# Own taps of a row LSTM as three products, with new gate blocks and a new written order

## The chip, the cores and the metric

The kernel runs on one core of a Trainium2 chip. The core has a matrix engine (TensorE, PE in the profile, with PEld for its weight loads), a vector engine (VectorE, DVE), an activation engine (ScalarE, ACT), a general engine (GpSimd, POOL) and a queue that starts DMAs (SyncE, SP). Each engine works off its own list of instructions in the order in which they stand, and waits at its head on semaphores that the other engines raise. The metric is the device time of one execution in microseconds (us); for the kernel before it is 1970.99 us (median of 3 runs, 1969.05 to 1977.06).

## The reference

A group normalisation of the input is followed by a row LSTM: a masked convolution of each image row gives the input part of four gates, a 3-tap convolution of the previous row's hidden state gives the other part, and the result is added to the input.

```python
# x: (8, 96, 128, 128); W_is: (384, 96, 1, 3); W_ss: (384, 96, 3)
# mask: tap 2 is zero; of tap 1 the first third of the outputs sees inputs 0:32,
# the second third 0:64, the last third all 96; tap 0 is whole
its = conv(group_norm(x), W_is * mask)          # along the row, padding 1
def step((h, c), row_in):                       # one image row, h and c (8, 96, 128)
    gates = conv(h, W_ss) + row_in              # 3 taps along the row
    g5 = gates.reshape(B, 3, 4, 32, 128)        # 3 thirds of channels, 4 gates
    f, i, o = sigmoid(g5[:, :, 0]), sigmoid(g5[:, :, 1]), sigmoid(g5[:, :, 2])
    g = tanh(g5[:, :, 3])
    c = f * c + i * g
    h = o * tanh(c)
    return (h, c), h
out = x + moveaxis(scan(step, (0, 0), rows of its), 0, 2)
```

All of it is 32-bit floating point.

## The kernel before

**Two half-steps in flight.** The 8 images are two groups s = 0, 1 of 4. One half-step n is one image row of one group; there are 256, and consecutive half-steps belong to different groups, so that one can be in its products while the other is in its gates. A row of 128 pixels is held as 64 even and 64 odd pixels; 4 images by 64 pairs make the 256 columns of nearly every instruction.

**Products.** The 384 gate channels are three blocks A, B, C of 128, each in a bank of PSUM (tiles `ps0`, `ps1`, `ps2`), with the even pixels in the first half of a bank and the odd ones in the second. The three taps of the hidden state are four products per block for two pixels: `1` (moving operand `vs`, the sum of even and odd h) and `2` (`vf`, their difference), then `0` and `3` (`vd`, differences with the neighbours). The input part has three more: `P`, `Q`, `E`, from the group's 64 own input channels in `xs`; the other 32 channels lie beside h in the rows of the h products. After `1`, `2`, `P`, `Q` come for each block `cp` (ACT copies the first half of the bank with the bias to `m`, line 569), `lo` (DVE: first half = m + second, line 573) and `hi` (DVE: second half = m - second, line 577). `0` and `E` are added on top of the first half, `3` on top of the second.

**Lanes.** A matmul of 128 rows is cut into two pieces of 64 rows, and each piece into two instructions of 64 output columns, so that four 64x64 tiles of the array work at once (`n_split`, line 453, and `mm`, line 485). The two row halves are called lanes here; a bank may be written by one lane at a time, and `Lanes.wait` makes PE wait for its own earlier products when the lane changes.

**Gates.** In block A lie the 96 forget gates and a third of g, in B the input gates and a third of g, in C the output gates and the last third. `si` is a sigmoid (line 593), `ta` a tanh (line 581), `fg` the product of forget gate and cell (DVE, line 598), `gt` that of input gate and g (line 605 on POOL for even pixels, 607 on DVE for odd ones), `ce` the new cell (617), `th` its tanh (622), `ou` the new h (630), `F` and `S` the operands `vf` and `vs` (649, 645), `D` the operand `vd` (POOL, line 653), `re` the sum with the input (671).

**What sets the order.** It is written by hand. The body of the loop over half-steps 2 to 253 is the string `PERIOD` (line 781), so there are 252 bodies. In it `'` marks the previous half-step, `''` the one before that, `+` the next; `<` and `>` name a lane; each product stands twice, once for each lane; a last letter a or b means even or odd pixels. `X` and `U` normalise the shared channels of a later row block (line 320 on POOL, 318 on ACT), `W1` to `W3` widen, add and subtract the own channels (320, 337, 341 on POOL). The half-steps ahead of the loop run during the pass that loads the input for its statistics, and the last ones have a list of their own (`LAST`). Waits between engines are set from the tiles that an instruction reads and writes; a bank is one tile there.

Rows arrive through SP: `load` (line 165) brings 4 rows of a group for the residual, `load_rows` (line 157) the own channels, twice, to 64 partitions each.

## Time and profile before

| | |
|---|---|
| median of 3 runs | 1970.99 us (1969.05 to 1977.06) |
| the profiled execution's own time | 1972.7 us |
| its span, first to last instruction | 1970.9 us |
| mean granted TensorE clock | 0.999 |
| instructions | 80552 |

How to read it: busy time of an engine is the union of its instructions' times. One matmul of the program on 32-bit data is two MATMUL records, one for each pass. In a row of the timeline stand the start, the time, the engine, the line of the kernel, the operation, the tiles written and read, the shape, and in brackets how long the engine stood idle just before and what ended that; neighbouring rows of the same form are merged, with their count behind x. In a row of the groups stand count, busy time, mean ns of one, and the idle time before them.

### The profile page before, as it was taken

The numbers are of one execution on the slowest core, as the hardware profiler recorded it, in microseconds if no ns is written. First come the engines' busy times: TensorE is split into PE (matmuls) and PEld (weight loads), VectorE is DVE, ScalarE is ACT, GpSimd is POOL, SyncE is SP. The second block draws the span as 40 slices with busy tenths as digits, with TensorE's granted clock in tenths as the row PEclk, the third lists the DMA queues.
The fourth block names the chain that finished last, engine by engine and source line by source line (L and its number), as shares of the span: only waits on it lengthen the run. The fifth ranks groups of instructions, "written<-read, shape, count | busy, mean of one in ns | idle before, by whom it ended". The sixth has DMA issues, their size and how long they took to land.

```text
span 1970.9 us, 80552 instructions
## 1 busy us (share of the span) xinstructions
PE 1904.7 (97%) x34510; PEld 1686.7 (86%) x34510; DVE 1801.1 (91%) x4014; ACT 1565.9 (79%) x3501; POOL 1360.3 (69%) x1645
## 2 busy tenths in 40 slices
PE   3799999999999999999999999999999999999998
PEld 0368999999999888888888999998888888988886
DVE  5888999999999999999999999999999899999998
ACT  6688888888888888787887878887888788877786
POOL 3457777777777777777777777777777777777751
PEclk9999999999999999999999999999999999999999
DMA  9993433544444345444434444443454444344411
GB/s 402 420 306 92 111 96 85 120 112 106 99 104 109 79 112 120 98 104 98 105 84 112 117 102 98 104 106 82 114 120 98 99 104 107 85 109 118 100 35 34
DMA packets 101428, 236.83 MB, mean 120 GB/s; under 512 B 5840, under 2 KB 7376, under 8 KB 95056
## 3 DMA queue, kind: packets, MB, share of 16 engines
q1 hardware_dynamic: 101072, 231.70, 45.2%
q8 instruction: 271, 4.44, 1.0%
q14 instruction: 85, 0.70, 0.1%
HBM read 181.34 MB, written 50.33 MB: 118 GB/s over the span
## 4 chain that ended last, share of the span: by engine, by line
PE 93%; DMA 3%; ACT 2%; DVE 1%; issue 1%; POOL 0%; SPq 0%; POOLq 0%; DVEq 0%; ACTq 0%
PE ps L498 92%; DMA xs<-in_x_dram 3%; DVE bst L1119 1%; ACT xs L239 0%; ACT xs L240 0%; ACT g L581 0%; PE rows L198 0%; ACT ps L593 0%; ACT piece L239 0%; DVE hx L630 0%; PE pv L274 0%; POOL xw L320 0%; DVE c L617 0%; SPq L1106 0%; ACT xr L208 0%
## 5 line engine op out<-in xcount | busy, mean ns | idle before, releaser
L498 PE MATMUL ps<-vd,wl 64*64 64x256 f32 (+1 forms) x12096 | 1208.9, 376 | 8.0 <-issue 5.1
L498 PE MATMUL ps<-vs,wm 64*64 64x256 f32 (+1 forms) x6058 | 832.9, 376 | 3.0 <-issue 1.6
L498 PEld LDWEIGHTS ps<-vd,wl 64*64 64x64 f32 (+1 forms) x12096 | 714.2, 133 | 81.2 <-issue 11.5
L498 PE MATMUL ps<-vf,wm 64*64 64x256 f32 (+1 forms) x6058 | 777.1, 376 | 1.5 <-issue 1.2
L498 PE MATMUL ps<-xs,wx 64*64 64x256 f32 (+2 forms) x7096 | 759.0, 346 | 1.8 <-POOL xs L337 1.8
L593 ACT ACTIVATE ps<-ps 96x512 f32<-96x512 f32 (+1 forms) x768 | 388.2, 506 | 227.0 <-PE ps L498 218.6
L498 PEld LDWEIGHTS ps<-xs,wx 64*64 64x64 f32 (+1 forms) x7096 | 483.6, 133 | 17.9 <-POOL xs L337 3.3
L581 ACT ACTIVATE g<-ps 32x256 f32<-32x256 f32 (+1 forms) x1021 | 469.2, 482 | 24.3 <-PE ps L498 3.2
L498 PE MATMUL ps<-xs,wt 64*64 64x256 f32 (+1 forms) x3024 | 458.3, 376 | 0.1
L569 ACT ACTIVATE m<-ps,wl 128x256 f32<-128x256 f32 x766 | 363.0, 474 | 107.6 <-PE ps L498 81.0
L498 PEld LDWEIGHTS ps<-vs,wm 64*64 64x64 f32 (+1 forms) x6058 | 409.3, 132 | 42.0 <-POOL vs L645 2.5
L653 POOL TENSOR_TENSOR vd<-hx 128x512 f32<-128x512 f32 x257 | 287.9, 1120 | 177.2 <-DVE vs L645 168.9
L498 PEld LDWEIGHTS ps<-vf,wm 64*64 64x64 f32 (+1 forms) x6058 | 355.8, 132 | 60.9 <-DVE vf L649 1.8
L573 DVE TENSOR_TENSOR ps<-m,ps 128x256 f32<-128x256 f32 x768 | 324.2, 422 | 81.1 <-ACT m L569 74.8
L577 DVE TENSOR_TENSOR ps<-m,ps 128x256 f32<-128x256 f32 x768 | 327.1, 426 | 17.7
L671 DVE TENSOR_TENSOR x<-x,hx 96x512 f32<-96x512 f32 x253 | 341.8, 1351 | 0.0
L320 POOL TENSOR_SCALAR xw<-xr,rstd,nmr 128x512 f32<-128x512 f32 (+1 forms) x264 | 210.2, 797 | 129.1 <-DVE x L671 116.0
L320 POOL TENSOR_SCALAR hx<-x,rstd,nmr 32x512 f32<-32x512 f32 (+1 forms) x244 | 220.9, 905 | 77.6 <-POOL xs L341 52.9
L341 POOL TENSOR_TENSOR xs<-xw 128x512 f32<-128x512 f32 (+1 forms) x254 | 271.5, 1069 | 0.0
L605 POOL TENSOR_TENSOR g<-i,g 96x256 f32<-96x256 f32 x251 | 183.2, 730 | 125.6 <-ACT g L581 116.9
L498 PEld LDWEIGHTS ps<-xs,wt 64*64 64x64 f32 (+1 forms) x3024 | 210.6, 133 | 2.5 <-issue 0.9
L617 DVE TENSOR_TENSOR c<-ps,g 96x256 f32<-96x256 f32 (+1 forms) x507 | 190.9, 416 | 7.7 <-POOL g L605 0.5
(101 smaller groups left out, 1502.8 us busy)
## 6 DMA issues: line engine op xcount, KB each, us to landing
xr<-in_x_dram SPq DMA_DIRECT2D x124, 512.0 KB, 7.0
x<-in_x_dram SPq DMA_DIRECT2D x62, 768.0 KB, 7.8
out_dram<-x SPq DMA_DIRECT2D x62, 768.0 KB, 5.0
xs<-in_x_dram SPq DMA_DIRECT2D x31, 1024.0 KB, 10.9
piece<-in_x_dram SPq DMA_DIRECT2D x16, 1024.0 KB, 10.8
x<-in_x_dram SPq DMA_DIRECT2D x62, 256.0 KB, 5.4
out_dram<-x SPq DMA_DIRECT2D x2, 576.0 KB, 3.9
xs<-in_x_dram SPq DMA_DIRECT2D x2, 512.0 KB, 10.0
```

What stands on the lines that cost most here:

```text
L320: return engine.tensor_scalar(dst, src, scale, shift, ALU.mult, ALU.add)
L341: engine.tensor_sub(differences, strided(xw[:, 0, :], 0, [(W + 1, n), (J, 2), (1, J)]), strided(xw[:, 0, :], J + 1, [(W + 1, n), (0, 2), ( ...
L498: made = nc.tensor.matmul(self.ps[a][bass.ts(q, wide), bass.ts(half, HB)][:, cols], weights[rows, bass.ds(a * P + q * wide, wide)], rhs[ro ...
L569: nc.scalar.activation(self.m1[a], m1, AF.Identity, bias=column)
L573: nc.vector.tensor_add(self.ps[a][:, 0:HB], self.m1[a], self.ps[a][:, HB:])
L577: nc.vector.tensor_sub(hi, self.m1[a], hi)
L581: nc.scalar.activation(self.part(g, lo, hi, t), self.part(ps, lo, hi, t), AF.Tanh)
L593: nc.scalar.activation(to, gate, AF.Sigmoid)
L605: nc.gpsimd.tensor_mul(to, i, g)
L617: nc.vector.tensor_add(c, f, g)
L653: diff = nc.gpsimd.tensor_sub(self.operand("vd", 2)[:, :, lo:hi], strided(h, 1, [(BH * JP - 1, 2), (JP, hi - lo), (1, J)]), strided(h, 0, ...
L671: residuals.append(nc.vector.tensor_add(xo, xo, self.h))
```

## The change

The own products are laid out anew. With the even pixel e, the odd pixel o and the odd pixel of the pair to the left, the outputs are written as P (both tap weights times e, for both pixels), E (left tap times the left neighbour's difference, even pixels) and Q (centre tap times o - e, odd pixels). The centre tap is masked, so Q is made for two column halves alone: columns 64 to 127 of block A and 0 to 63 of block B, one instruction each. The rest of Q, for input channels 0 to 31, takes the 32 free rows of product `3`: `ride` (token `K`) copies those rows of Q beside the third operand. For that the gate channels are permuted (A: forget gates and a third of g; B: two thirds and a third of the input gates and a third of the output gates; C: two thirds of the output gates and of g), and the own channels become 64..95 and 0..31, the shared ones 32..63.

With it go: the gates of B are read by `iu`, `il` and `so` instead of one `si` and one `ta`; `D` becomes `Z` (128x256) and `V` (96x256); `W2` (the addition of pixels) is dropped and `W2` names the subtraction; the loads of own channels are four of 32 partitions instead of two of 64; the first rows have picking products and a bank of their own; the strings `PERIOD` and `LAST` are written anew.

```diff
+    wq = const.tile([P, 2, O4], F32, name="wq")
-    wo = [wx[:, 0, :], wx[:, 1, :], tap[3]]
...
     def load_rows(s, k, lo=0, hi=R):
-        src = rows_of(s, k, 0, C2, lo, hi)
-        for p in range(2):
-            nc.sync.dma_start(xr[s][p * C2 : (p + 1) * C2, :, lo * W : hi * W], src)
+        for p in range(4):
+            c0 = 0 if p % 2 else 64
+            nc.sync.dma_start(
+                xr[s][p * 32 : (p + 1) * 32, :, lo * W : hi * W],
+                rows_of(s, k, c0, c0 + 32, lo, hi),
+            )
...
         if i == 0:
-            first[b] = bank(f"rows{b}")
+            first[b], own_first[b] = bank(f"rows{b}"), bank(f"own{b}")
...
-    def add_pixels(xw, n, total, engine=nc.gpsimd):
-
-        engine.tensor_add(total, xw[:, 0:n, 0:J], xw[:, 0:n, J + 1 :])
...
         "1": (0, 1, ("vs", 0)),
         "2": (1, 2, ("vf", 0)),
-        "0": (0, 0, ("vd", 1)),
-        "3": (1, 3, ("vd", 0)),
+        "0": (0, 0, ("vz", 0)),
+        "3": (1, 3, ("vr", 0)),
...
+            if lane is not None:
+                lane ^= self.n % 2
+            if kind == "Q":
+                rows = lanes.take(lane=lane)
+                for a, q in ((0, 1), (1, 0)):
+                    self.images[a] = (0, BH)
+                    self.mm(a, 1, wo[kind], self.at_rows(kind), rows, (q,))
+                return True
...
-            if t == 0 and NH < self.n < last:
-                self.even_input = self.tile("i", (C, HB))
...
+        def output_gate(self, lo=0, hi=BH, t=None):
+            gate, to = self.ps[1][32:C2], self.ps[2][C2:C]
...
+        def input_upper(self, lo=0, hi=BH, t=None):
+            nc.scalar.activation(
+                self.part(self.i[0:C2], lo, hi, t), self.part(self.ps[1][C2:P], lo, hi, t), AF.Sigmoid
+            )
+
+        def input_lower(self, lo=0, hi=BH, t=None):
+            nc.scalar.activation(
+                self.part(self.i[C2:C], lo, hi, t), self.part(self.ps[1][0:32], lo, hi, t), AF.Sigmoid
+            )
...
+        def ride(self, lo=0, hi=BH):
+            nc.gpsimd.tensor_copy(
+                self.operand("vr")[C:P, 0, lo:hi], self.at_rows("Q")[C:P, lo:hi]
+            )
...
     PERIOD = (
-        "1B> 3C'< D'' 2A> 0C'< 1A> siBa' 2B< 3C'> 1B< EC'> 2C< taA' 0C'> re'' 1C< fg' taB' PB+> "
-        "PC+< cpA W1 loA cpB 1C> hiA loB hiB siBb' QCl+< taCa' taCb' EA< 2C> gtb' W2 3A< siC' "
-        "0B> gta' 0A< cpC 3B> QA+< W3 cea' tha' EB> PA+< ceb' loC 0A> 0B< oua' thb' oub' X F' "
-        "3A< 3B> QB*> S' 2A+< 2B+> 1A+< U QCh+> siA hiC"
+        "1B< U F 2A> X W1' 2B< siA' ilb' Z re'' fg' taCb' V 1C> 0C'> taA' 1B> 1A< iub' gtb' "
+        "cpB cpA 2B> 1C< 0C'< 2A< loB PC+< loA 2C< cpC hiB PB+< 0B< K+ hiA ceb' taCa' 2C> "
+        "gta' loC 0A< 3B> EA< so' siC' 0B> 3A< thb' EB> PA+> cea' hiC oub' QA> tha' EC< oua' "
+        "0A> 3C< S+ 3A> 3B< 3C> iua 1A+> ila W2'"
     )
...
     perm = np.concatenate(
-        [np.concatenate([idx[:, a].reshape(-1), idx[a, 3]]) for a in range(3)]
+        [
+            idx[k, gate]
+            for k, gate in (
+                (0, 0), (1, 0), (2, 0), (2, 3),
+                (2, 1), (2, 2), (0, 1), (1, 1),
+                (0, 2), (1, 2), (0, 3), (1, 3),
+            )
+        ]
     )
```

Two places show how the instructions stand. The names are tiles: `ps0`, `ps1`, `ps2` are the banks of blocks A, B, C, followed by group, row and a number; `wl_64`, `wm_66`, `wx_67`, `wt2_65` are weights; `x2` is the pair of column halves; in brackets is the engine whose semaphore the instruction waits for. `Lanes` is behind a wait of PE on PE.

PE before, at the end of the products `1` and `2` of half-step (row 42, group 0) with pieces of `0`, `3` and `E` of the half-step ahead of it between them:

```order
L498 MATMUL ps1_0_42_10410<-vf_0_42_10528,wm_66 64x256 [waits PE_49]
L498 MATMUL ps1_0_42_10410<-vf_0_42_10528,wm_66 64x256
L498 MATMUL ps2_1_40_10343<-vd_1_40_10430,wl_64 64x256 [waits PE_49]
L498 MATMUL ps2_1_40_10343<-vd_1_40_10430,wl_64 64x256
L498 MATMUL ps1_0_42_10410<-vs_0_42_10537,wm_66 64x256 x2
L498 MATMUL ps2_1_40_10343<-xs10_76,wt2_65 64x256 x2
L498 MATMUL ps2_0_42_10468<-vf_0_42_10528,wm_66 64x256 x2
L498 MATMUL ps2_1_40_10343<-vd_1_40_10430,wl_64 64x256 x2
L498 MATMUL ps2_0_42_10468<-vs_0_42_10537,wm_66 64x256 x2
```

Here PE waits for itself alone. PE in the changed kernel, from the last piece of `3B` of half-step (row 41, group 0) over the products `1` and `2` of (row 40, group 1) to the second pieces of `2B` and `2A`:

```order
L495 MATMUL ps1_0_41_10332<-vr_0_41_10337,wl_64 64x256
L495 MATMUL ps2_0_41_10323<-vr_0_41_10337,wl_64 64x256 [waits PE_49]
...
L495 MATMUL ps2_1_40_10444<-vs_1_40_10502,wm_66 64x256 x2
L495 MATMUL ps2_0_41_10323<-vz_0_41_10409,wl_64 64x256 [waits Activation_49]
...
L495 MATMUL ps1_1_40_10453<-vs_1_40_10502,wm_66 64x256
L495 MATMUL ps0_1_40_10485<-vs_1_40_10502,wm_66 64x256 x2
L495 MATMUL ps1_1_40_10453<-vf_1_40_10520,wm_66 64x256 [waits Activation_49]
...
L495 MATMUL ps2_0_41_10323<-vz_0_41_10409,wl_64 64x256 [waits PE_49]
L495 MATMUL ps2_0_41_10323<-vz_0_41_10409,wl_64 64x256
L495 MATMUL ps0_1_40_10485<-vf_1_40_10520,wm_66 64x256 [waits Activation_49]
```

The second pieces of `2B` and `2A` now stand behind a copy of the same bank by ACT, and the first piece of `0C` behind a tanh of bank C.

ACT before, from the copy of block C over a body's gates to the copies of A and B:

```order
L569 ACTIVATE m2_0_59_14761<-ps2_0_59_14604,wl_64 128x256 [waits PE_49]
L622 ACTIVATE th_1_57_14770<-c1_83 96x256 [waits DVE_49] x2
L593 ACTIVATE ps0_0_59_14642<-ps0_0_59_14642 96x512 [waits PE_49]
L593 ACTIVATE i_0_59_14822<-ps1_0_59_14550 96x256 [waits PE_49,Pool_49]
L581 ACTIVATE g_0_59_14836<-ps0_0_59_14642 32x512 [waits Activation_49]
L581 ACTIVATE g_0_59_14836<-ps1_0_59_14550 32x512
L569 ACTIVATE m0_1_58_14850<-ps0_1_58_14765,wl_64 128x256 [waits PE_49]
L569 ACTIVATE m1_1_58_14854<-ps1_1_58_14673,wl_64 128x256 [waits PE_49]
```

ACT in the changed kernel, from the first input gate (`iua`) to the copies of B and A; `X` is the row with L332:

```order
L622 ACTIVATE i_0_62_15646<-ps1_0_62_15467 64x256 [waits PE_49,Pool_49]
L627 ACTIVATE i_0_62_15646<-ps1_0_62_15467 32x256
L332 ACTIVATE hx10_73<-x1_16_15424,nmr1_105,rstd1_103 32x2x64 [waits DMAHW6_49,Pool_49]
L607 ACTIVATE ps0_0_62_15499<-ps0_0_62_15499 96x512
L627 ACTIVATE i_0_62_15646<-ps1_0_62_15467 32x256
L601 ACTIVATE g_0_62_15669<-ps2_0_62_15458 64x256 [waits DVE_49,PE_49]
L601 ACTIVATE g_0_62_15669<-ps0_0_62_15499 32x512 [waits DVE_49]
L622 ACTIVATE i_0_62_15646<-ps1_0_62_15467 64x256
L588 ACTIVATE m1_1_61_15684<-ps1_1_61_15587,wl_64 128x256 [waits PE_49]
L588 ACTIVATE m0_1_61_15686<-ps0_1_61_15619,wl_64 128x256 [waits PE_49]
```

The sigmoid of block A stood first of a body's gates and now stands behind two input gates of block B; seven gate instructions stand ahead of the copies, where there were four.

## The prediction

> **What bounds the kernel now.** I read the page first: the busy times, and the chain that ended last.

> ```profile
> PE 1904.7 (97%) x34510; PEld 1686.7 (86%) x34510; DVE 1801.1 (91%) x4014; ACT 1565.9 (79%) x3501; POOL 1360.3 (69%) x1645
> ...
> PE ps L498 92%; DMA xs<-in_x_dram 3%; DVE bst L1119 1%; ACT xs L239 0%; ACT xs L240 0%; ACT g L581 0%; PE rows L198 0%; ACT ps L593 0%; ACT piece L239 0%; DVE hx L630 0%; PE pv L274 0%; POOL xw L320 0%; DVE c L617 0%; SPq L1106 0%; ACT xr L208 0%
> ...
> L593 ACT ACTIVATE ps<-ps 96x512 f32<-96x512 f32 (+1 forms) x768 | 388.2, 506 | 227.0 <-PE ps L498 218.6
> ```

> 92% of the chain is products into the banks, and ACT waits 218.6 us for them before its sigmoids. Whether busy PE is full PE shows in the timeline of one body.

> ```profile
> 1003.14 0.38 PE L498 MATMUL ps<-vd,wl 64*64 64x256 f32 x2
> 1003.21 0.38 PE L498 MATMUL ps<-vf,wm 64*64 64x256 f32 x2
> 1003.36 0.38 PE L498 MATMUL ps<-vd,wl 64*64 64x256 f32 x2
> 1003.43 0.38 PE L498 MATMUL ps<-vs,wm 64*64 64x256 f32 x2
> 1003.57 0.38 PE L498 MATMUL ps<-vf,wm 64*64 64x256 f32 x2
> ...
> 1001.63 0.42 DVE L645 TENSOR_TENSOR vs<-hx 128x256 f32<-128x256 f32 x1
> 1001.97 0.42 DVE L577 TENSOR_TENSOR ps<-m,ps 128x256 f32<-128x256 f32 x1
> 1002.30 1.53 DVE L671 TENSOR_TENSOR x<-x,hx 96x512 f32<-96x512 f32 x1
> 1009.42 1.52 DVE L671 TENSOR_TENSOR x<-x,hx 96x512 f32<-96x512 f32 x1
> ```

> A lane starts a pair of records every 0.215 us (1003.14, 1003.36, 1003.57), the other lane in between; a piece of two passes holds its lane for 0.43 us and ends 0.215 + 0.38 = 0.59 us after its start. A body has 66 instructions of 64 columns, 33 to a lane pair and pass: 33 x 0.215 = 7.10 us, and the residual of one body follows that of the last after 7.12. PE never stands still, and the period is its work. The busy times of a stretch of the loop, times 7.12/400, give those of a body: DVE 6.65, ACT 5.75, POOL 5.24.

> ```profile
> 400.00:800.00 400.00, 400.00 (x7632) 365.13 (x7626) 373.50 (x843) 323.24 (x743) 294.50 (x336) 1.00 0.44 104
> ```

> **The change part by part.**

> *Products.* 66 instructions become 62 (Q two instead of six; the h products stay 48). If PE stayed full: 31 x 0.215 + 0.02 = 6.69 us, 0.43 less, over 252 bodies 108 us.

> *ACT.* These are its rows in a body, and the tail, where PE no longer covers the waits:

> ```profile
> 1001.70 0.57 ACT L593 ACTIVATE ps<-ps 96x512 f32<-96x512 f32 x1 [0.98 <-PE ps L498]
> 1002.19 0.37 ACT L593 ACTIVATE i<-ps 96x256 f32<-96x256 f32 x1
> 1002.59 1.22 ACT L581 ACTIVATE g<-ps 32x512 f32<-32x512 f32 x2
> 1004.08 1.05 ACT L569 ACTIVATE m<-ps,wl 128x256 f32<-128x256 f32 x2 [0.27 <-PE ps L498]
> 1005.02 0.37 ACT L593 ACTIVATE ps<-ps 96x256 f32<-96x256 f32 x1
> 1005.42 0.65 ACT L581 ACTIVATE g<-ps 32x256 f32<-32x256 f32 x2
> 1006.10 0.57 ACT L593 ACTIVATE ps<-ps 96x512 f32<-96x512 f32 x1
> 1006.70 0.47 ACT L569 ACTIVATE m<-ps,wl 128x256 f32<-128x256 f32 x1
> ...
> 1014.21 0.75 ACT L622 ACTIVATE th<-c 96x256 f32<-96x256 f32 x2
> 1014.99 0.50 ACT L318 ACTIVATE hx<-x,nmr,rstd 32x128 f32<-32x128 f32 x1
> ```

> ```profile
> 1958.26 0.59 PE L498 MATMUL ps<-vf,wm 128*128 128x256 f32 x2
> ...
> 1958.90 0.48 DVE L567 TENSOR_SCALAR m<-ps,wl 128x256 f32<-128x256 f32 x1 [0.62 <-PE ps L498]
> 1959.42 0.43 DVE L573 TENSOR_TENSOR ps<-m,ps 128x256 f32<-128x256 f32 x1
> 1959.88 0.43 DVE L577 TENSOR_TENSOR ps<-m,ps 128x256 f32<-128x256 f32 x1
> ...
> 1960.45 3.19 PE L498 MATMUL ps<-vd,wl 128*128 128x256 f32 x12
> ...
> 1962.28 0.57 ACT L593 ACTIVATE ps<-ps 96x512 f32<-96x512 f32 x1
> 1962.88 0.59 ACT L581 ACTIVATE g<-ps 32x512 f32<-32x512 f32 x1
> 1962.88 0.69 DVE L598 TENSOR_TENSOR ps<-ps,c 96x512 f32<-96x512 f32 x1 [0.49 <-ACT ps L593]
> ```

> An instruction of 256 columns costs 0.37 us whether it has 32 or 96 partitions, so cutting a gate by partitions adds instructions and saves nothing: per body 13 become 15, two more of 256 columns at 0.28 to 0.40 us. ACT idles 0.98 + 0.27 us in the shown body, so by load alone it would still fit 6.69. By place it does not. In the new lists there is a loop that closes once per body, and I add it up from the rows, beginning with the last piece of `3B`:

> 1. The piece ends after 0.59, and ACT starts `iua` some 0.05 later (1958.26 + 0.59 to 1958.90 is PE to DVE): 0.64.
> 2. `iua` and `ila` stand ahead of `siA` on ACT: two of 256 columns back to back, spaced 0.65 - 0.37 = 0.28: 0.56.
> 3. `siA` to `fg`: 1962.28 to 1962.88, 0.60.
> 4. `fg` 0.69 + 0.03 to `taA`, which reads the same bank: 0.72.
> 5. `taA` to `iub`: half of the 1.22 for two, 0.61.
> 6. `iub` to `cpB`: as 1002.19 to 1002.59 (a sigmoid, then another function), 0.40.
> 7. `cpB` 0.47, then the second piece of `2B` waits for it. No row shows PE released by ACT; bounds are 0.05 (PE to DVE) and 0.14 (DVE to PE, 1959.88 + 0.43 to 1960.45); I take the middle, 0.10: 0.57.
> 8. `2B` holds its lane 0.43, behind it go a piece of `0C` and that of `2A`; `2A` ends 0.59 + 0.05 later at `loA`: 1.07.
> 9. `loA` stands ahead of `hiB` on DVE and delays it by a slot, 0.34 (1001.63 to 1001.97 above, where nothing is waited for); `hiB` 0.43 + 0.10 to `0B`: 0.87.
> 10. From the first piece of `0B` to the last of `3B` its lane has seven pieces (`0A`, `E` of A, `3A`, `P` of the next half-step, `E` of C, `3C`, then `3B`): 7 x 0.43 = 3.01.

> Sum 9.05 us. `X` (0.50, one body in four, between `ila` and `siA`; next start some 0.45 later) adds 0.11: 9.16 us per body, against 6.69 of work on PE. Before, every second piece of `1` and `2` stood ahead of the copies, so no such loop closed through PE. The wait of `0C` for `taCb` and that of bank `P` for `so` lie beside this loop.

> *DVE.* Its 15 instructions stay. What changes is who reads SBUF: `gt` for odd pixels takes i from SBUF instead of a bank.

> ```profile
> 1002.23 1.04 POOL L653 TENSOR_TENSOR vd<-hx 128x512 f32<-128x512 f32 x1 [0.92 <-DVE vs L645]
> ...
> 1957.59 0.68 DVE L671 TENSOR_TENSOR x<-x,hx 96x512 f32<-96x512 f32 x1
> ...
> L337 POOL TENSOR_TENSOR xs<-xw 128x256 f32<-128x256 f32 x252 | 161.9, 643 | 20.8
> L341 POOL TENSOR_TENSOR xs<-xw 128x512 f32<-128x512 f32 x252 | 270.3, 1073 | 0.0
> L320 POOL TENSOR_SCALAR xw<-xr,rstd,nmr 128x512 f32<-128x512 f32 x245 | 201.8, 824 | 116.2 <-DVE x L671 116.0
> L607 DVE TENSOR_TENSOR g<-ps,g 96x256 f32<-96x256 f32 x255 | 105.5, 414 | 3.7 <-ACT g L581 2.2 <-ACT ps L593 1.4
> ```

> `re` takes 0.68 us where it starts before POOL's `D` and 1.53 where `D` (1.04) started 0.07 ahead: it ends 0.56 after `D` does. So an operation of DVE with both inputs in SBUF stands until POOL's is done. With `Z` of half the size (0.64 by the addition of that size) `re` falls to about 1.13, and `gt` may rise from 0.41 to at most 1.48 behind the subtraction (1.07). DVE's 6.65 us per body then become 6.2 to 7.3, inside 9.16: no term. [...]

> *POOL.* Out goes the addition (0.64) and `D` (1.04 to 1.12); in come `Z` and `V` (0.64 each) and the copy `K` (32x256, no row; between 0 and the 0.64 of an addition of that width). Net 0.64 + 0.64 + K - 0.64 - 1.04, so -0.4 to +0.24 us on 5.24. `V` and the subtraction now wait for `re`; `3B` needs `V` only 4 us into a body. Free at 9.16 us; at 6.69 it would not be.

> *SP, start, end, restarts.*

> ```profile
> xr<-in_x_dram SPq DMA_DIRECT2D x124, 512.0 KB, 7.0
> ...
> L198 PE MATMUL rows<-xs,pick 128*128 128x512 f32 x32 | 27.1, 942 | 32.4 <-DMA xs<-in_x_dram 32.3
> ...
> L498 PEld LDWEIGHTS ps<-xs,wx 64*64 64x64 f32 x7028 | 475.4, 133 | 10.7 <-issue 0.6 <-ACT th L622 0.3
> ```

> The 124 loads become 248 of half the size; they land 7 us after their issue and are issued a block of four rows (8 bodies, 57 us) ahead: nothing, unless the queue itself were late. The load pass gets 24 more picking products, each of two records of some 0.9 us in which PE otherwise waits 32.3 us for DMA: 0 to 20 us, taken as 0, since each follows one that waits for the same piece. The tail has four more ACT instructions at 0.4: under 2 us.

> **Sum.** The profiled execution took 1972.7 us, of which 252 x 7.12 = 1794 are bodies. Now 252 x (9.16 - 7.12) = +514, so 2487; against the median (1.7 lower) 2485 us.

> **Rivals.**

> *A, the loop does not close, and PE stays full: faster.* It decides at one point: ACT would have to bring `cpB` before PE wants the second `2B`. From the last `3B` piece PE has seven starts in two lanes until `0C` (1.46 us), and three more until `2B`, 2.1 us; ACT needs steps 1 to 7, 4.1 us. For it speaks that PE is full now and loses 6% of its work; against it that nothing in ACT's list can be overtaken. It would give 6.69, so 1972.7 - 108 = 1864, or, if POOL (5.2 to 5.5) and DVE's two-input operations (`re` 0.68, `F` and `S` 0.34 each, `gt` 0.34; 1.7) exclude each other wholly, 7.0 us and 1942. 4 in 100.

> *B, a shorter loop.* If PE's second pieces started without waiting for the copies, steps 7 and 8 become `cpA` behind `cpB` (0.39) and 0.50 to `loA`: 9.16 - 0.57 - 1.07 + 0.89 = 8.41 us, 2298. The list has the waits written down, which speaks against it. 4 in 100.

> *C, a longer one.* Each restart of PE costs more than its wait (a weight load of 133 ns ahead of the first product, at `2B`, `0B`, `0C` and `2C`): +0.5 us per body, 2612. The 0.14 in step 7's bound already holds one such load. 6 in 100.

> *D, no change within 0.5%:* an accident between these, 1 in 100.

> **How the numbers follow.** My forecast has 85 in 100. Its own range: steps 7 and 9 at 0.05 or 0.14 (-0.10, +0.08), step 6 at 0.28 (-0.12), DVE not free for `fg` because `re` is late (+0.2): 8.9 to 9.4 us, 2420 to 2545. I widen it to 2400 and 2560 for the start and the products I could not price; that leaves out A, B, C and D, 15 in 100. Runs of this kernel differ by 0.4%, so about 0.5% can be told from none. Faster 0.04, same 0.01, slower 0.95.

> **What would show it.** In the changed profile: residuals 9.0 to 9.3 us apart; PE busy near three quarters of the span and no longer nearly all of the chain, which should go through ACT's L622, L627, L607 and L588, DVE's L634 and L597 and PE; idle time of PE put down to ACT `m` L588; `siA` starting with no wait of its own right behind `ila`; `re` near 1.1 us. Wrong would be a period under 8 us, or a chain that is PE alone (A), or PE's idle time ended by DVE or POOL, not by ACT.

## The result, and the profile after

| | before | changed |
|---|---|---|
| median of the runs | 1971.57 us (1969.05 to 1977.06, 4 runs) | 2641.78 us (2640.54 to 2643.06, 4 runs) |
| the profiled execution, its span | 1972.7, 1970.9 us | 2641.73, 2640.0 us |
| mean granted TensorE clock | 0.999 | 0.975 |

The changed kernel is slower by a ratio of 1.339 (95% interval 1.337 to 1.342). The prediction said 2485 us, with 2400 to 2560 as its range: the direction and the place of the loss are as it said, the size is not. The page of the changed kernel (busy times, then the chain that ended last by engine and by line):

```profile
PE 2172.9 (82%) x31566; PEld 1559.0 (59%) x31566; DVE 1671.4 (63%) x4024; ACT 1746.0 (66%) x4001; POOL 1416.2 (54%) x1913
...
ACT 32%; PE 32%; DVE 27%; issue 5%; DMA 2%; POOL 0%; DVEq 0%; SPq 0%; ACTq 0%; POOLq 0%
PE ps L495 31%; ACT g L601 9%; ACT m L588 7%; DVE ps L593 5%; DVE ps L634 5%; ACT ps L607 4%; ACT i L622 4%; ACT i L627 4%; DVE hx L663 4%; DVE x L717 4%; DVE ps L597 3%; ACT ps L611 3%; DMA xs<-in_x_dram 2%; DVE vf L682 2%; DVE vs L678 2%
```

No engine is busy for more than 82% of the span, and the chain, which was PE for 92% before, now passes between ACT, PE and DVE in nearly equal shares. That is a loop through three engines, as forecast. The waits of the changed kernel, in all, with their number and the longest:

```profile
ACT i L622 <- PE ps L495: 419.1, 252, 2.3
...
PE ps L495 <- ACT g L601: 242.3, 250, 2.3
...
PE ps L495 <- ACT m L588: 118.8, 250, 7.0
```

Each of them comes some 250 times, once per body. `iua` (L622) waits for the last piece of `3B`; PE waits for the tanh `taCb` (L601) ahead of `0C`, and for the copy `cpB` (L588) ahead of `2B`.

**One body of the changed kernel.** The timeline of a body without `X`, from one `iua` to the next (ACT, DVE and PE rows of the loop, in the order of time):

```profile
1557.03 0.68 DVE L717 TENSOR_TENSOR x<-x,hx 96x512 f32<-96x512 f32 x1
1557.43 0.38 ACT L622 ACTIVATE i<-ps 64x256 f32<-64x256 f32 x1 [1.62 <-PE ps L495]
1557.82 0.37 ACT L627 ACTIVATE i<-ps 32x256 f32<-32x256 f32 x1
1558.10 0.57 ACT L607 ACTIVATE ps<-ps 96x512 f32<-96x512 f32 x1
1558.70 0.70 DVE L634 TENSOR_TENSOR ps<-ps,c 96x512 f32<-96x512 f32 x1 [0.99 <-PE ps L495]
1559.00 1.03 ACT L601 ACTIVATE g<-ps 64x256 f32<-64x256 f32 x2
1559.43 0.43 PE L495 MATMUL ps<-vz,wl 64*64 64x256 f32 x2 [0.76 <-ACT g L601]
1560.04 0.38 ACT L622 ACTIVATE i<-ps 64x256 f32<-64x256 f32 x1
1560.44 0.84 ACT L588 ACTIVATE m<-ps,wl 128x256 f32<-128x256 f32 x2
1560.97 0.43 PE L495 MATMUL ps<-vf,wm 64*64 64x256 f32 x2 [0.46 <-ACT m L588]
1561.23 0.38 PE L495 MATMUL ps<-vf,wm 64*64 64x256 f32 x2
1561.68 0.38 PE L495 MATMUL ps<-vf,wm 64*64 64x256 f32 x2
1561.73 0.94 DVE L593 TENSOR_TENSOR ps<-m,ps 128x256 f32<-128x256 f32 x2 [0.87 <-PE ps L495]
1562.59 0.75 DVE L597 TENSOR_TENSOR ps<-m,ps 128x256 f32<-128x256 f32 x2
1563.16 0.43 PE L495 MATMUL ps<-vz,wl 64*64 64x256 f32 x2 [0.24 <-DVE ps L597]
1566.62 0.69 DVE L717 TENSOR_TENSOR x<-x,hx 96x512 f32<-96x512 f32 x1
1566.95 0.39 ACT L622 ACTIVATE i<-ps 64x256 f32<-64x256 f32 x1 [1.68 <-PE ps L495]
```

The starts give the loop term by term, each as the difference of two starts:

| steps of the prediction | forecast us | measured us |
|---|---|---|
| 2: `iua`, `ila` ahead of `siA` (1557.43 to 1558.10) | 0.56 | 0.67 |
| 3: `siA` to `fg` (to 1558.70) | 0.60 | 0.60 |
| 4, 5: `fg`, `taA`, to `iub` (to 1560.04) | 1.33 | 1.34 |
| 6: `iub` to `cpB` (to 1560.44) | 0.40 | 0.40 |
| 7: `cpB` to the second `2B` (to 1560.97) | 0.57 | 0.53 |
| 8, 9: to `0B`, over `loB`, `loA`, `hiB` (to 1563.16) | 1.94 | 2.19 |
| 10, 1: seven lane pieces, the last `3B`, to `iua` (to 1566.95) | 3.65 | 3.79 |
| sum | 9.05 | 9.52 |

So the loop is there with its steps, and 0.47 us longer: 252 x 0.47 = 118 us. The bodies with `X` (at full clock) are some 10.0 us long instead of 9.5, 63 x 0.47 = 30 us, of which the prediction had 28.

**A second loss that the prediction did not have.** Some bodies with `X` take 11.1 us. Here are two residuals of such a body and PE's first rows in it, and then stretches of the same execution (busy time of each engine, then the granted clock, the DMA share and GB/s):

```profile
1576.15 0.71 DVE L717 TENSOR_TENSOR x<-x,hx 96x512 f32<-96x512 f32 x1
1579.10 0.43 PE L495 MATMUL ps<-vz,wl 64*64 64x256 f32 x2 [1.43 <-ACT g L601]
...
1579.38 0.80 PE L495 MATMUL ps<-vs,wm 64*64 64x256 f32 x6
1580.60 0.43 PE L495 MATMUL ps<-vf,wm 64*64 64x256 f32 x2 [0.42 <-ACT m L588]
...
1581.42 0.65 PE L495 MATMUL ps<-vf,wm 64*64 64x256 f32 x2
1581.85 0.64 PE L495 MATMUL ps<-vf,wm 64*64 64x256 f32 x2
...
1587.19 0.69 DVE L717 TENSOR_TENSOR x<-x,hx 96x512 f32<-96x512 f32 x1
```

```profile
160.00:180.00 20.00, 11.99 (x136) 7.53 (x140) 8.04 (x19) 11.32 (x24) 6.88 (x9) 0.70 0.25 54
1200.00:1600.00 400.00, 333.72 (x5086) 242.76 (x5084) 252.62 (x615) 265.84 (x625) 223.25 (x288) 0.98 0.30 75
1577.78:1581.19 3.41, 1.67 (x24) 1.01 (x28) 1.12 (x2) 3.02 (x7) 1.72 (x3) 1.00 0.00 0
1581.19:1584.60 3.41, 3.41 (x38) 2.24 (x34) 1.84 (x5) 1.54 (x4) 0.68 (x1) 0.50 0.02 5
1656.28:1659.69 3.41, 1.84 (x28) 1.13 (x32) 1.12 (x2) 2.85 (x7) 1.54 (x3) 1.00 0.00 0
1659.69:1663.10 3.41, 3.17 (x55) 2.28 (x48) 2.95 (x9) 2.49 (x6) 1.52 (x2) 1.00 0.02 5
```

Behind two waits of PE, 1.43 and 0.42 us, the granted clock falls to 0.50 for 3.41 us (the expectations say 0.53 for 3.6 us, from wider bounds), and the passes of PE start 0.43 us apart (1581.42, 1581.85) instead of 0.215. Behind the twelfth body 23 bodies have such a stretch, all of them bodies with `X`; by the starts of the residuals they are 10.9 to 11.6 us long, so each loses about 1.1 us, 25 us in all. (The expectations below say 28, from a rougher first count.)

The clock's own entries in the trace say which bodies are hit. Every stretch of half clock that ends before the kernel does is 3.41 us long or a multiple of it, and the starts lie whole multiples of 3.41 us apart: the clock changes on a fixed grid of windows, wherever the bodies stand on it. In the changed kernel behind the twelfth body each of the 23 windows at full clock in which PE was busy for at most 1.82 of 3.41 us is followed by one at half clock (the pair from 1577.78 on), and none of the other 641, in which it was busy for 1.84 us or more (the pair from 1656.28 on). So a body is hit when enough of its two waits falls into one window.

At the start the clock is low too (0.70 from 160 to 180 us), where the first bodies take 16.2 and 12.5 us.

2485 + 118 (loop) + 2 (`X`) + 25 (half clock) leaves 12 us of 2642, which the first bodies account for (6.6 + 2.9 + 2.8 us above 9.5 in three of them). Two smaller terms are not in this sum and nearly cancel. The first residual comes 8.6 us later (156.6 us against 148.0), where the prediction took 0, out of 0 to 20, for the load pass. And the kernel before has six bodies of 8.4 to 9.1 us in its loop, some 10 us above the 7.12 of the others; the prediction carried them over, and the bodies of the changed kernel show no such extra. What makes them long was not taken apart.

### The profile page after: what moved, and what is told of

The parts are those of the page before. It is cut to its first block, busy times and chain, and to the rows that moved or that the text cites. A ratio compares the mean times of both kernels' runs of the same rounds, so it can differ in the third digit from the quotient of the medians.

```text
span 2640.0 us, 77597 instructions
## 1 busy us (share of the span) xinstructions
PE 2172.9 (82%) x31566; PEld 1559.0 (59%) x31566; DVE 1671.4 (63%) x4024; ACT 1746.0 (66%) x4001; POOL 1416.2 (54%) x1913
## 4 chain that ended last, share of the span: by engine, by line
ACT 32%; PE 32%; DVE 27%; issue 5%; DMA 2%; POOL 0%; DVEq 0%; SPq 0%; ACTq 0%; POOLq 0%
PE ps L495 31%; ACT g L601 9%; ACT m L588 7%; DVE ps L593 5%; DVE ps L634 5%; ACT ps L607 4%; ACT i L622 4%; ACT i L627 4%; DVE hx L663 4%; DVE x L717 4%; DVE ps L597 3%; ACT ps L611 3%; DMA xs<-in_x_dram 2%; DVE vf L682 2%; DVE vs L678 2%
## 5 line engine op out<-in xcount | busy, mean ns | idle before, releaser
L495 PE MATMUL ps<-vz,wl 64*64 64x256 f32 (+1 forms) x6048 | 931.7, 392 | 299.6 <-ACT g L601 242.3
L495 PE MATMUL ps<-vf,wm 64*64 64x256 f32 (+1 forms) x6058 | 833.1, 396 | 118.9 <-ACT m L588 118.8
L495 PEld LDWEIGHTS ps<-vz,wl 64*64 64x64 f32 (+1 forms) x6048 | 439.8, 135 | 553.7 <-ACT g L601 356.2
L495 PE MATMUL ps<-vr,wl 64*64 64x256 f32 (+1 forms) x6054 | 655.1, 379 | 0.0
L588 ACT ACTIVATE m<-ps,wl 128x256 f32<-128x256 f32 x766 | 335.2, 471 | 361.2 <-PE ps L495 354.8
L593 DVE TENSOR_TENSOR ps<-m,ps 128x256 f32<-128x256 f32 x768 | 329.1, 429 | 363.1 <-PE ps L495 257.5
L495 PE MATMUL ps<-xs,wx 64*64 64x256 f32 (+1 forms) x4050 | 540.3, 390 | 3.8 <-ACT ps L611 2.9
L622 ACT ACTIVATE i<-ps 64x256 f32<-64x256 f32 (+1 forms) x509 | 194.4, 382 | 422.1 <-PE ps L495 419.1
L495 PEld LDWEIGHTS ps<-vr,wl 64*64 64x64 f32 (+1 forms) x6054 | 404.4, 132 | 58.4 <-issue 0.6
L495 PEld LDWEIGHTS ps<-xs,wx 64*64 64x64 f32 (+1 forms) x4050 | 306.7, 137 | 108.3 <-issue 13.8
L601 ACT ACTIVATE g<-ps 64x256 f32<-64x256 f32 (+1 forms) x765 | 345.0, 451 | 25.4 <-DVE ps L597 0.5
L634 DVE TENSOR_TENSOR ps<-ps,c 96x512 f32<-96x512 f32 x254 | 176.7, 696 | 281.1 <-ACT ps L607 247.3
L688 POOL TENSOR_TENSOR vz<-hx 128x256 f32<-128x256 f32 x257 | 234.4, 912 | 221.3 <-PE ps L495 147.1
L351 POOL TENSOR_TENSOR xs<-xs 128x512 f32<-128x512 f32 (+1 forms) x255 | 322.6, 1266 | 1.4 <-ACT xs L332 0.6
L597 DVE TENSOR_TENSOR ps<-m,ps 128x256 f32<-128x256 f32 x768 | 299.4, 420 | 0.4
L607 ACT ACTIVATE ps<-ps 96x512 f32<-96x512 f32 (+1 forms) x510 | 290.0, 569 | 8.2
## 6 DMA issues: line engine op xcount, KB each, us to landing
xs<-in_x_dram SPq DMA_DIRECT2D x2, 512.0 KB, 6.5
```

Of the source, the lines that this page charges most:

```text
L351: return engine.tensor_sub(strided(base, 0, [(step, n), (2 * J + 1, 2), (1, J)]), strided(base, 2 * J, [(step, n), (1, 2), (1, J)]), strid ...
L495: made = nc.tensor.matmul(to[bass.ts(q, wide), images], weights[rows, bass.ds(a * P + q * wide, wide)], rhs[rows, images], start=new, stop ...
L588: nc.scalar.activation(self.m1[a], m1, AF.Identity, bias=column)
L593: nc.vector.tensor_add(self.ps[a][:, 0:HB], self.m1[a], self.ps[a][:, HB:])
L597: nc.vector.tensor_sub(hi, self.m1[a], hi)
L601: nc.scalar.activation(self.part(g, lo, hi, t), self.part(ps, lo, hi, t), AF.Tanh)
```

## The experiments

Each ran beside the kernel before on the same chip; the ratio is to that kernel.

| run | median us | ratio (95% interval) |
|---|---|---|
| changed kernel | 2641.78 | 1.339 (1.337 to 1.342) |
| e1: `X` behind the copies | 2570.74 | 1.302 (1.299 to 1.305) |
| e2: `iua`, `ila` behind the copies | 2388.89 | 1.209 (1.207 to 1.212) |
| e3: second pieces of `2B`, `2A` ahead of the copies | 2427.50 | 1.229 (1.226 to 1.231) |
| e4: e1, e2 and e3 together | 2252.77 | 1.140 (1.138 to 1.143) |
| e5: order of before, new products and gates | 2153.26 | 1.091 (1.089 to 1.094) |
| e6: kernel before, with cut gates alone | 2056.41 | 1.043 (1.041 to 1.045) |
| e7: an `X` in every body | 2757.00 | 1.397 (1.395 to 1.399) |
| e8: `hiB` ahead of `loA` | 2612.64 | 1.325 (1.322 to 1.328) |
| e9: e5 with input gates of 512 columns | 2177.86 | 1.104 (1.102 to 1.106) |
| e10: another order | 2153.84 | 1.092 (1.090 to 1.093) |
| e11: another order, `cpA` on DVE | 2186.53 | 1.108 (1.107 to 1.110) |

### e1: is `X` on the path, and whose is the half clock?

```diff
-        "1B< U F 2A> X W1' 2B< siA' ilb' ... cpB cpA 2B> 1C< ..."
+        "1B< U F 2A> W1' 2B< siA' ilb' ... cpB cpA X 2B> 1C< ..."
```

> Edit: the token X (normalisation of shared channels on ACT, one body in four) goes from ahead of the gates to behind the copy cpA, where ACT stands idle 1.29 us in the changed kernel. Loop theory: X delays siA and all behind it by 0.40 us in 63 bodies, 25 us. In about 28 bodies with X (one in eight) the residuals of the changed kernel are 11.1 us apart instead of 10.0, and in one such body the granted clock reads 0.53 for 3.6 us behind a wait of PE of 1.43 us. If that wait is what halves the clock, X gone makes the wait 0.76 as in the other bodies and another 28 us go: 2642 - 53 = 2589 us, mean clock from 0.975 to about 1.0. Rival: the half clock belongs to the row block's loads and stores, which fall on the same bodies; then 2617 us and the clock stays at 0.975. If X is not on the path at all: 2642.

2570.74 us, 71 less, where 53 were expected with the half clock gone. The stretch 1200 to 1600 us of this run:

```profile
1200.00:1600.00 400.00, 336.72 (x5209) 245.62 (x5208) 259.08 (x631) 272.52 (x643) 229.31 (x295) 1.00 0.32 79
```

The clock is 1.00 there, 0.98 in the changed kernel. Behind the twelfth body a single one has a stretch of half clock; nearly all others are 9.4 to 9.7 us long. The transfers of the row blocks are the same as before the edit, so they are not what halves the clock. The 18 us beyond that are partly at the start (the first body takes 10.4 us, not 16.2).

### e2: step 2, `iua` and `ila` off the loop

```diff
-        "... iub' gtb' cpB cpA 2B> 1C< ... 3B< 3C> iua 1A+> ila W2'"
+        "... iub' gtb' cpB cpA iua' ila' 2B> 1C< ... 3B< 3C> 1A+> W2'"
```

> Edit: iua and ila, which stand ahead of siA on ACT, go behind the copies cpB and cpA of the next body (the list of the last half-steps gets them too). Loop theory: step 2 of the prediction leaves the loop; in the changed kernel it measures 0.39 + 0.28 = 0.67 us per body, 169 us over 252 bodies, and with PE's wait in the bodies with X shorter by as much the half clock there goes too (28 us): 2642 - 197 = 2445 us, 2473 if the half clock stays. Rival: ACT's whole list or the cut of the gates itself sets the body (same instructions, same engine): 2642 within 1%.

2388.89 us: 253 less, against 197. Bodies without `X` fall from 9.53 to 8.78 us, by 0.75 instead of 0.67; bodies with `X` are no longer longer (8.7 to 8.9 all), since `X` now lies in `siA`'s wait for PE; and the half clock is gone (the granted clock reads 1.00 in each stretch of 400 us from 400 to 2000). Together 0.75 x 252 = 189, 30 for `X` and 25, 244 of the 253. The rival, that ACT's list as such sets the body, falls: the list has the same instructions.

### e3: steps 7 and 8, PE without the wait for the copies

```diff
-        "... taA' 1B> 1A< iub' gtb' cpB cpA 2B> 1C< 0C'< 2A< loB ..."
+        "... taA' 1B> 1A< 2B> 2A< iub' gtb' cpB cpA 1C< 0C'< loB ..."
```

> Edit: the second pieces of 2B and 2A go ahead of the copies cpB and cpA, so that PE no longer waits for ACT there; nothing else moves. Loop theory: from the start of cpB to that of loA the changed kernel takes 0.53 + 0.75 + 0.52 = 1.80 us over PE (steps 7 and 8); without PE it is cpA behind cpB and loA behind cpA, 0.39 + 0.47 + 0.05 = 0.91. So 0.89 us less per body, 224 us, and 28 more if the half clock goes: 2418 or 2390. Rival: PE's restarts are the cost and only move to the next wait (0B behind hiB): then at most the 0.43 of one piece goes, 108 us, 2534. Rival without a loop: 2642.

2427.50 us: 214 less, where 224 to 252 were expected. Bodies without `X` take 8.78 us, 0.75 less; those with it mostly 9.3 to 9.4. From the start of `cpB` to that of `loA` it is 0.91 us, as expected, but `cpB` now waits for PE, with the second piece of `2B` ahead of it, and starts 0.55 us behind `iub` instead of 0.40 (1223.35 to 1223.90 in a body of this run), so 0.89 - 0.15 = 0.74 is left:

```profile
1223.35 0.38 ACT L622 ACTIVATE i<-ps 64x256 f32<-64x256 f32 x1
1223.90 0.87 ACT L588 ACTIVATE m<-ps,wl 128x256 f32<-128x256 f32 x2 [0.17 <-PE ps L495]
```

The half clock is gone (1.00 in each stretch of 400 us from 400 to 2000) although PE's wait ahead of `0C` is as long as it was. Here are PE's waits in a body with `X` of this run:

```profile
1214.03 0.43 PE L495 MATMUL ps<-vz,wl 64*64 64x256 f32 x2 [1.44 <-ACT g L601]
1217.00 0.43 PE L495 MATMUL ps<-vz,wl 64*64 64x256 f32 x2 [0.53 <-DVE ps L597]
```

In place of the wait for the copy, 1.08 us behind the first one in the changed kernel (1579.10 to 1579.38 + 0.80), stands one for `hiB`, and between it and the first wait PE works for 2.4 us (1214.03 to 1217.00 - 0.53). So a wait of 1.44 us alone does not halve the clock.

### e4: do the parts add up?

> Edit: the three moves together (second pieces of 2B and 2A ahead of the copies, iua and ila behind them, X behind these). Loop theory, if the parts add up: 0.89 + 0.67 us per body and the 53 us of X: 2642 - 224 - 169 - 53 = 2196 us. If another wait closes in their place (the first piece of 0C behind the tanh taCb of the same bank, by now ahead of four pieces that the copies wait for): between 2196 and 2390. Under the rival that the cut gates load ACT too much for any order: not under 2390.

The edit is e1, e2 and e3 in one list. 2252.77 us, 57 over the plain sum and inside the expected range: 389 us less, where the three alone gave 71 + 253 + 214 = 538. Of those, the half clock (25 us) is in all three and the cost of `X` (30) in two, 80 us too many; the other 69 say that the two waits of the loop do not come off one by one. The chain of this run is mostly PE again:

```profile
PE 60%; DVE 21%; ACT 12%; issue 4%; DMA 3%; POOL 0%; SPq 0%; DVEq 0%; ACTq 0%; POOLq 0%
```

### e5: order or layout?

```diff
-        "1B< U F 2A> X W1' 2B< siA' ilb' Z re'' fg' taCb' V 1C> 0C'> taA' 1B> 1A< iub' gtb' "
...
+        "1B> 3C'< Z V 2A> 0C'< 1A> iua' ila' 2B< 3C'> 1B< EC'> 2C< taA' 0C'> re'' 1C< fg' PB+> "
+        "PC+< cpA W1' loA cpB 1C> hiA loB hiB ilb' iub' taCa' taCb' EA< 2C> gtb' so' 3A< siC' 0B> "
+        "gta' 0A< cpC 3B> K+ W2' cea' tha' EB> PA+< ceb' loC 0A> 0B< oua' thb' oub' X F+ 3A< 3B> "
+        "QA< S+ 2A+< 2B+> 1A+< U siA hiC"
```

> Edit: the changed kernel's products, gates and layout stay, its written order goes; PERIOD is the list of before with the new tokens put where their forerunners stood (copies cpA and cpB behind PE's second pieces, iua and ila where siBa was, Z and V where D was, lanes as in the list of before). Theory that the order makes the loss: PE no longer waits for copies, and the body is set either by PE (16 pieces in the fuller lane, 16 x 0.43 = 6.88 us, 1912 us in all) or by ACT's list (from the slots of the run with the three moves: 7.0 us, 1945) or, since cpB now stands ahead of all later gates, by the loop cpB, ilb, iub, taCa, taCb, so, siC, cpC, th, ou, F, 2A to 1B and cpB again, some 7.9 us by its rows: 2170. So under 2200. Rival, the new products and cut gates make the loss in any order: not under the 2253 of the three moves.

2153.26 us, with 7.87 us between residuals; 7.9 and 2170 were expected. (Lanes no longer change with the half-step's parity, and the list of the last half-steps finishes what this order leaves.) So 489 of the 670 us that the change costs are its written order, and 181 stay with the order of before. The loop that was expected runs through `F`, and the waits fit it: from 400 to 1600 us PE waits for `vf` in every body, though in a stretch of 400 us it is busy for 397. That just this loop sets the body is not shown, since e9, which takes `ilb` and `iub` out of it, gained nothing.

```profile
PEld ps L495 <- DVE vf L680: 79.5, 153, 0.5
```

```profile
1200.00:1600.00 400.00, 396.95 (x6308) 301.24 (x6308) 352.00 (x765) 325.69 (x776) 294.02 (x356) 1.00 0.38 95
```

### e6: one part alone, the cut gates in the kernel before

```diff
+            if a == 1 and t is not None and NH < self.n < last:
...
+                for p0, p1 in ((0, C2), (C2, C)):
+                    gate = self.part(self.ps[a][p0:p1], lo, hi, t)
...
+                    nc.scalar.activation(to, gate, AF.Sigmoid)
+                return
```

> Edit: the kernel before, with one part of the change alone: each of the two sigmoids of block B (96 partitions) is cut into two of 64 and 32 partitions, so ACT has two more instructions of 256 columns per body, 15 instead of 13. They add 0.28 to 0.40 us each. Theory that a cut gate costs only where the order puts it on the path: PE's 7.12 us per body stay, 1975 us within 0.5%, since ACT stood idle 0.98 + 0.27 us in a body. Rival, ACT's longer list is itself the loss: 252 x 0.56 = 141 us more, 2115 us.

2056.41 us: 84 more than before, between the two theories, and clearly not the none that I expected. Residuals are 7.47 us apart instead of 7.12. PE hardly waits for `vf` in the kernel before, and in nearly every body here; the row of its waits in the kernel before, and in this one:

```profile
PEld ps L498 <- DVE vf L649: 1.8, 5, 0.6
```

```profile
PEld ps L498 <- DVE vf L659: 125.0, 244, 0.7
```

By these waits two more sigmoids of 256 columns, on an engine that stood idle 0.98 + 0.27 us per body, delay everything behind them on ACT up to the new h and with it `F`. The idle time lay ahead of `siA` and of the copies, not where the added work stands.

### e7: the half clock with the wait in every body

```diff
+                if name == "X" and not any(p[1] is nc.scalar for p in worked[n - NH][0]):
+                    nc.scalar.activation(
+                        pad[C:P], wl[C:P, 0:W], AF.Identity, bias=bias[C:P, 0:1], scale=bias[C:P, 1:2]
+                    )
```

> Edit: the changed kernel with an instruction of the form of X on ACT in every body, not in one of four: where a body has no X, an Identity of 32x128 on constants is written to a tile that nobody reads, at the same place ahead of siA. So PE's wait ahead of 0C becomes 1.43 us in all bodies instead of one in four. Theory: each of the other 189 bodies grows by 0.47 us (10.0 against 9.53), 89 us; and if the half clock comes of PE's waits alone (28 of 63 bodies with X have it now, 1.05 us each), it comes as often in the others: 189 x 28/63 x 1.05 = 88 us more: 2642 + 177 = 2819 us, mean clock 0.92. Rival, the half clock belongs to the row block's transfers: 2731 us and a clock near 0.975.

2757.00 us, between the two numbers. The plain bodies grew to 10.1 us, as expected (the median rises by 0.54; 189 x 0.54 = 102 us). Stretches of half clock now come at any place of a row block, 33 behind the twelfth body, where they came on bodies with `X` alone before. The stretch 1200 to 1600 us:

```profile
1200.00:1600.00 400.00, 320.68 (x4840) 230.57 (x4840) 241.78 (x586) 269.60 (x626) 212.97 (x274) 0.97 0.29 73
```

So the half clock belongs to PE's waits and not to the transfers, but the wait alone does not suffice: with it in every body the drop came in 33 of 240 bodies, while of the 58 with `X` in the changed kernel it hit 23. Where the waits stand on the grid of 3.41 us decides it here as well: in this run 33 windows with PE busy for up to 1.85 us are followed by half clock, and none of 654 with more. The expected size was wrong by 62 us, since it took the share of hit bodies over from the bodies with `X` without that grid.

### e8: step 9, `loA` ahead of `hiB`

```diff
-        "... loB PC+< loA 2C< cpC hiB PB+< 0B< K+ hiA ..."
+        "... loB PC+< hiB loA 2C< cpC PB+< 0B< K+ hiA ..."
```

> Edit: in the changed kernel hiB goes ahead of loA on DVE (step 9 of the prediction: loA stands ahead of hiB and delays it). From loB to loA it takes 0.52 us in the changed kernel, then 0.34 to hiB. If the loop runs through DVE alone there, 0.52 us per body go, 130 us, and 28 with the half clock: 2512 or 2484 us. But PE is idle only 0.24 us ahead of 0B; if its own pieces behind 2A (PC, 2C, PB) hold it from then on, only that goes: 60 us, 2582 us, or 2554 with the half clock. If step 9 is not on the loop: 2642.

2612.64 us, 29 less; by the smaller of the two expected gains 60 or 88 would have gone. `hiB`, `loA` and `hiA` on DVE, and PE, in a body of this run:

```profile
1077.99 0.43 PE L495 MATMUL ps<-vf,wm 64*64 64x256 f32 x2 [0.46 <-ACT m L588]
...
1079.22 0.43 DVE L597 TENSOR_TENSOR ps<-m,ps 128x256 f32<-128x256 f32 x1
1079.56 0.42 DVE L593 TENSOR_TENSOR ps<-m,ps 128x256 f32<-128x256 f32 x1
1079.80 0.65 PE L495 MATMUL ps<-vz,wl 64*64 64x256 f32 x4
1080.02 0.43 DVE L597 TENSOR_TENSOR ps<-m,ps 128x256 f32<-128x256 f32 x1
...
1080.50 0.43 PE L495 MATMUL ps<-vz,wl 64*64 64x256 f32 x2
```

In the body of the changed kernel shown above `0A` is this row:

```profile
1563.61 0.63 PE L495 MATMUL ps<-vz,wl 64*64 64x256 f32 x4
```

`0B` starts 1.81 us behind `2B` (1077.99 to 1079.80) instead of 2.19 (1560.97 to 1563.16), without a wait. But the next product in its lane, `0A`, now has to wait for `hiA`, which ends at 1080.45: it starts 2.51 us behind `2B` (1080.50) where it was 2.64 (1563.61). In this pair of bodies 0.13 us are left. Over all bodies without `X` the length falls from 9.53 to 9.44 us, 0.09 x 252 = 23 us, and 16 bodies have half clock where 23 had it, 8 us. So the term of step 9 is on the loop, and taking it out gains little, since another instruction is next.

### e9, e10, e11: can the new products do better in another order?

e9 is e5 with `iu'` and `il'` for both pixels where `iua'`, `ila'`, `iub'` and `ilb'` were; e10 and e11 are lists in which copies, gates and pieces stand elsewhere altogether, in e11 with `cpA` on DVE:

```diff
+        "K X Z siA' 1A> 2B< V iua' iub' EC'> 1B< re'' 0C'> 2C< taA' cpA loA 3C'> 1C< PB+< cpB loB "
+        "2C> il' hiA taC' hiB 1C> fg' so' cpC 3B< gta' gtb' siC' 3A> cea' PC+< tha' EB> EA< ceb' "
...
-            if a == order["A"] and self.n in (1, last):
+            if a == order["A"] and (self.n in (1, last) or NH < self.n < last):
```

> Edit: the run with the old order, and in it the input gates of block B read for both pixels at once: iu and il of 512 columns where iua and ila stood, iub and ilb gone. ACT has two instructions less (13), the same columns. The run with the old order takes 7.87 us per body, and by its expected loop (cpB, ilb, iub, taCa, taCb, so, siC, cpC, th, ou, F, 2A to 1B and cpB) 0.40 + 0.40 us of it are ilb and iub. If that loop alone sets the body, they go from it: 7.07, 1952 us. If another wait closes before (iu and il take 0.60 each ahead of taA and the copies): between 1952 and 2153, a half of it, 2050, is my number. Rival, the cuts are not on the path in that order: 2153.

> Edit: the changed kernel's products and gates in another order altogether: copies stand behind all pieces of 1 and 2 of their block, iua and iub ahead of the copies, il and taC read both pixels at once, PC and PA late. Theory that order makes the loss: under 2153, some 7.4 us per body (between PE's 6.88 and the 7.87 of the old order): 2040 us. Rival, that the layout as such costs the 181 us that the old order leaves: 2153 or more. Under 1972 it would beat the kernel before.

> Edit: another order again, with the copy cpA on DVE in place of ACT (one instruction of 0.48 us in each body goes from ACT to DVE). If ACT's list is what the new layout pays with, the body falls to 7.0 to 7.4 us: 1935 to 2040 us. If DVE, with 6.2 us of work per body and two-input operations that stand behind POOL's, is by then as tight as ACT: 2040 to 2153.

2177.86, 2153.84 and 2186.53 us: all three missed their number. e9 and e11 lie above everything that was expected, and e10 lies where its rival had it (2153 or more). Two instructions less on ACT, with the same columns, made e9 slower by 25 us than e5, so ACT's count is not what holds e5. e11 has both another order and the copy on DVE; what each of them did is not told apart. e10, with an order of its own, ends at the 7.87 us of e5, and no run explains why two so different orders end within 0.01 us of each other. Its stretch of 400 us, and the head of its chain:

```profile
1200.00:1600.00 400.00, 400.00 (x6309) 320.71 (x6300) 330.69 (x765) 320.55 (x675) 286.14 (x356) 1.00 0.38 95
```

```profile
PE 95%; DMA 2%; DVE 1%; ACT 1%; POOL 0%; issue 0%; SPq 0%; POOLq 0%; DVEq 0%; ACTq 0%
```

PE is busy for all of the 400 us and is 95% of the chain, and still a body of 31 starts per lane pair and pass takes 7.87 us, where 31 x 0.215 = 6.67. Its two lanes are not full all the time. The waits of this run show PE behind its own other lane in a bank once per body:

```profile
PEld ps L495 <- PE ps L495: 92.7, 256, 0.5
```

That is 0.36 of the 1.2 us per body; the remainder is not taken apart. No order that was run beats the kernel before. What part of the 181 us the layout must cost, and what part is an order not found, stays open; in the kernel before, the cut gates alone cost 84 (e6).

## Why the prediction was right and wrong

**The step that failed: the size of the loop.** The place and the order of the loop are right. Its sum is 0.47 us short per body, 118 of the 157 us that are missing, in steps 2, 8 to 10 and 1; and the clock of PE, 25 us, is not in the sum at all.

**What bounds it: right.** PE full before, a loop through ACT, DVE and PE afterwards that closes once per body: the chain, the three engines' idle time and the table of terms show it, and e2 and e3, which each take a part out of it, gain 0.75 us per body each. e5 shows that the order makes 489 of 670 us.

**Steps 3 to 7: right** to 0.04 us, `siA` right behind `ila` without a wait of its own included. Step 7's 0.57, a middle between bounds, measured 0.53.

**Step 2: too small** by 0.11. The two gates were priced as back to back, 0.28 each; `ila` starts 0.39 behind `iua` and `siA` 0.28 behind `ila`. In the body shown the first ACT instruction behind the wait for PE does not overlap the next. Moved off the loop, the two gave 0.75 (e2).

**Steps 8 and 9: too small** by 0.25. The prediction had `loA` 0.05 behind the end of `2A`, by one row of the tail, and then two slots of DVE. Measured, `loB` starts 0.76 behind `2B` and `loA` 0.52 behind that, 1.28 where it had 1.07. Of these 0.21, 0.07 are PE's: the first passes behind a wait are further apart than in a full stream (1560.97 to the next pass at 1561.23 is 0.26, not 0.215), and the last pass of `2A` starts 0.71 behind the first of `2B` (1561.68), where three slots make 0.645. The other 0.14 are the start of DVE: the pass of `2A` ends at 1562.06 by the profile, whose ends of matmuls are modelled, and `loA` starts 0.19 later, not 0.05; in nine of ten bodies that gap is 0.19, and for `loB` behind `2B` it is 0.12. `0B` starts 0.15 behind the end of `hiB`, where 0.10 was taken. e8 shows that here several chains end within 0.1 us of each other, so no single wait is the term; the 0.25 are read from starts and were not measured by a run of their own.

**Steps 10 and 1: too small** by 0.14, of 3.65. About 0.08 of it are slower passes again, behind `hiB`, and 0.06 the start of `iua`, which in most bodies comes 0.11 behind the end of the last `3B` and not 0.05.

**The first bodies and the half clock: missing,** 12 and 25 us. The prediction had PE idle for a quarter of the time and did not ask what that does to its clock. In e1 and e2 one of PE's two waits is shorter and in e3 the second is further off, and the half clock goes in all three but for one body of e1: on the grid of 3.41 us PE is then busy for at least 2.12, 2.35 and 1.96 us of a window, except for one window of e1 with 1.86, which is followed by that body's half clock, and one of e3 with 1.71, which is not. So near 1.85 us the busy time parts the windows, with single exceptions (in e8 one of 1.84 is not followed by half clock and one of 1.85 is); that another measure of PE's work would fit them all is not shown.

**Products: 0.43 us gained if PE stayed full: not shown.** e5 and e10 have PE busy for 99 and 100% of the time at 7.87 us per body, so with these products and lanes a busy PE is not 31 x 0.215. Rival A's 1864 us rested on that number.

**ACT fits by load alone: no guide to the cost.** The prediction found room on ACT for two more gates, and the expectation of e6 made of it that they cost nothing there. In e6 two cut gates cost 84 us, in an order where ACT had idle time. Idle time counts where it stands in the list.

**Rivals.** B, the loop without PE's waits for the copies, was priced at 8.41 against 9.16: 0.75 less. e3 is that edit, and it gains 0.75. The mechanism was right; that the price is the same is in part luck, since the stretch taken out measured 1.80 us where the prediction had 1.64, and the new wait of `cpB` for PE (0.15) made up for it. C, a longer loop by PE's restarts, gave 2612, the nearest number; its price of 0.5 us is what the loop was too short by, but for other reasons in the main: behind `cpB` PE starts 0.05 us after ACT, less than the 133 ns of a weight load, and the 0.47 us are made up of the gates of step 2, late starts of DVE and ACT behind PE, and slower first passes. No experiment changed restarts alone.

**DVE and POOL: wrong in who goes first, without weight.** `re` takes 0.68 us in the body shown, not 1.13: it starts before `Z`. The odd `gt` keeps its short time, and POOL's operations stretch instead:

```profile
L688 POOL TENSOR_TENSOR vz<-hx 128x256 f32<-128x256 f32 x257 | 234.4, 912 | 221.3 <-PE ps L495 147.1
L351 POOL TENSOR_TENSOR xs<-xs 128x512 f32<-128x512 f32 (+1 forms) x255 | 322.6, 1266 | 1.4 <-ACT xs L332 0.6
...
L640 DVE TENSOR_TENSOR g<-i,g 96x256 f32<-96x256 f32 (+1 forms) x256 | 108.9, 426 | 268.8 <-ACT i L622 267.0
```

`Z` takes 0.91 and the subtraction 1.27 us, where operations of that size took 0.64 and 1.07 before. In the kernel before, `re` took 1.48 to 1.55 us in the 184 bodies in which it started about 0.07 behind `D`, and ended some 0.56 after it; here `re` starts 0.23 ahead of `Z` as a rule and takes 0.69, and `Z` takes the longer time. So much is shown of this pair. That every operation of DVE with both inputs in SBUF stands until POOL's is done, as the prediction has it, is not shown: in 60 bodies of the kernel before `S` starts 0.18 to 0.24 behind POOL's `X` and takes its usual 0.42, and `X` takes 1.2 to 1.3 where it otherwise mostly takes 0.7 to 0.8. The 1.48 up to which the prediction let `gt` rise was its estimate; the mean is 0.43. Which of `re` and `Z` starts first the prediction got wrong, and it did not matter to the time.

**The other signs.** PE is busy for 83% of a stretch, not three quarters. Most of its idle time is ended by `taCb` L601 (242.3 us) and not by `cpB` L588 (118.8), which I had named as the sign; the terms in the table leave `taCb` out and still make up the body, as the prediction said of it. The finer loads, `xr` in 248 pieces, changed nothing that the chain shows.
